# Two cross-attentions: image outputs of all heads added on TensorE to the transposed text outputs

## The chip, the core and the metric

The kernel runs on one core of a Trainium2 chip. The metric is the device time of one execution in microseconds, as the median of repeated runs. The names of the engines in the profile: PE is TensorE's matmuls, PEld its weight loads, DVE is VectorE, ACT is ScalarE, POOL is GpSimd, SP is SyncE, which here only issues DMAs.

## What is computed

Two cross-attention layers run one after the other on 64 batches of 256 positions with 320 channels: 20 heads of 16 channels (D). The context of each batch has 77 tokens of 512 channels. The first layer attends to all 77 text tokens (its image slice is empty); for the second, 73 are text tokens and 4 are image tokens (NIP). In the second layer the image scores also take a cosine between the text-attended context and the image tokens. Cut to the part that the change touches:

```python
text_out = jnp.einsum('bhst,bhtd->bhsd', probs_t, v_t)
...
probs_ip = jax.nn.softmax(fused, axis=-1)
probs_ip = probs_ip * spatial_mask[None, None, :, None]
ip_out = jnp.einsum('bhsn,bhnd->bhsd', probs_ip, v_ip)
...
out = text_out + IP_SCALE * ip_out
out = out @ W_out + b_out
out = out + residual
```

All of it is in float32. The image part of the output is a weighted sum over only four tokens a head.

## The kernel before, in words

Batches go in pairs p (NP = 32 of them, each two batches b of 256 positions). The work of a pair is cut in ten units, five a batch, and one loop of steps g runs everything as a software pipeline: step g belongs to p = g // 10 and k = g % 10. In each step the first layer works on unit g and the second on unit g - 13 (LAG), and its products on the unit before that. All other work (projections, keys, loads, the image part) is a list of "fillers" that the function `fillers(k, p)` hangs on step k. Fillers of the second layer's end belong to pair p - 2. Each step emits, in this order: leftovers of the step before ("drains", kept in `held`), the products and scores into the score banks of PSUM (L769, L776, L654), fillers `begin`, VectorE's maximum and subtraction (L672, L674) for each layer, the transposes of the second layer's weights (L718, L719; copies L725, L726), fillers `first`, the products' sums (L787, L790, copy L1102), the transposes of the first layer's weights (the same L718, L719; copies L744, L745), fillers `second` and `third`. In steps 1, 6 and 8 the sums' copy (L1102) is emitted ahead of the first layer's transposes, in the others behind.

`keep_order` fixes that the instructions of PE, ACT, DVE and POOL run in the order in which they are emitted. SP's order is fixed so for the first 13 steps alone; after that the scheduler of the framework orders the DMA issues.

PSUM has eight banks: four for the scores (`psc`), two for `ptr` (tag "tr") and two for `pms` (tag "ms"). Each pool hands its two buffers out in turn, and a new tile waits until its buffer has been read out.

The path of the image outputs of pair p - 2 before the change:

- `text_output` (POOL, L895 through `by_head`): at the end of a batch (step 9 for b = 0, step 4 for b = 1) it writes the normalized text outputs. Heads 0 to 15 (HT) go to `an`, the last four heads of both batches to `an_last`, positions on the partitions.
- `text_transposed` (steps 0 and 5, `third`): four TensorE transposes of `an` (L856) and two ACT copies (L858) into `aT1`, channels on the partitions.
- `image_weights` (POOL) in steps 2 and 7 makes the image weights `iw` and `iw_last`. `image_transposed` (step 7, L952, copy L954) turns the weights of 16 heads, 64 rows, into `iwT`.
- `image_values` (steps 7 and 8) loads the image values of 16 heads by 16 DMAs a batch (L483), each the same four rows of `vip_rows`; `place_image_values` (POOL, step 9, L488) sets all but each head's own channels to zero.
- `image_attend` (step 8, after the scores): four matmuls a pair (L964), of 32 rows each, into two banks of `pms`; ACT copies them to `ip_out` (L974), POOL adds them to `aT1` (L976; for the last pair VectorE, L972).
- `last_image_values` loads the last four heads' values, broadcast over all partitions (L494); `last_image_outputs` (POOL, steps 4 and 7) multiplies and adds them token by token, eight instructions a batch (L867, L870), onto `an_last`; `last_transposed` (step 8) transposes `an_last` (L877) and ACT copies it (L880).
- `project(1, p - 2)` (step 9, L542) reads `aT1`; its end (L552, L612) follows in step 0.

Other names that the working uses: `value_rows` (L386, copy L387) projects rows of values in steps 6 and 8; `values` loads them back by batch into `vm` and `vr` or `v_rest` (L402), `place_values` spreads them on POOL (L431 to L471); `keys_by_head` (L372) follows it on POOL, and the copy `kT` (L344) waits for that.

Of the kernel before, what the change touches and what calls it, by code (L numbers as in the profile page):

```python
# [14 lines left out]
H = 20  # L15
# [55 lines left out]
def tile_two_cross_attentions(ctx: ExitStack, tc: tile.TileContext, a: dict, out: bass.AP):  # L71
# [182 lines left out]
    ip_mask = blocks("ip_mask", HT * NIP, HT, NIP)  # L254
# [21 lines left out]
    for b in range(2):  # L276
        nc.vector.memset(gv[b][:, :, :, GV - 1 :], 1.0)
        nc.vector.memset(gr[b], 0.0)
        nc.gpsimd.tensor_copy(
            gr[b][:, :, :, GR - 1 :], rest1.unsqueeze(1).unsqueeze(3).broadcast_to([P, 3, 2, 1])  # L280
        )

# [48 lines left out]
    kTs, kbds, qs, vips, aTs = {}, {}, {}, {}, {}  # L331
# [145 lines left out]
    def image_values(p, b):  # L477


        n, r0 = HT * NIP, (2 * p + b) * NIP  # L480
        vip = vips[p, b] = big.tile([n, 2 * P], F32, tag="vip", name=f"vip{p}_{b}", bufs=3)
        for h in range(HT):
            nc.sync.dma_start(vip[h * NIP : (h + 1) * NIP, :], vip_rows[r0 : r0 + NIP, : 2 * P])  # L483

    def place_image_values(p, b):
        n, vip = HT * NIP, vips[p, b]
        v = vip.rearrange("p (h d) -> p h d", d=D)
        nc.gpsimd.tensor_tensor(v, v, ip_mask[:n].unsqueeze(2).broadcast_to([n, HT, D]), ALU.mult)  # L488

    def last_image_values(p, b):  # L490

        r0 = (2 * p + b) * NIP
        v = vips[p, b, "last"] = small.tile([P, NIP, HALF], F32, tag="vlast", name=f"vlast{p}_{b}", bufs=1)
        nc.sync.dma_start(v, vip_rows[r0 : r0 + NIP, 2 * P :].unsqueeze(0).broadcast_to([P, NIP, HALF]))  # L494
# [338 lines left out]
    lasts = {}  # L833

    def text_output(p, b):

        sums = stats[p, b][1]
        rec = small.tile([P, 2 * H], F32, tag="rec", name=f"rec{p}_{b}", bufs=2)
        nc.vector.reciprocal(rec, sums[:, :, NIP + D])
        an = big.tile([P, 2, HT, D], F32, tag="an", name=f"an{p}_{b}", bufs=1)  # L840
        if b == 0:
            lasts[p] = big.tile([P, 2, 2, H - HT, D], F32, tag="an_last", name=f"an_last{p}", bufs=1)
        by_head(an, lasts[p][:, :, b], sums[:, :, NIP : NIP + D], rec)
        return an

    def text_transposed(p, b):

        an = made["an"]
        if b == 0:
            aTs[1, p] = channels("aT1", f"aT1_{p}", 1)  # L850
        main = aTs[1, p][0]
        for s in range(2):
            ps = ptr.tile([P, 4, P], F32, tag="tr", name=f"atr{p}_{b}{s}")
            t = an[:, s].rearrange("p h d -> p (h d)")
            for i in range(2):
                nc.tensor.transpose(ps[:, i, :], t[:, i * P : (i + 1) * P], ident)  # L856
            t0 = b * S + s * P
            nc.scalar.copy(main[:, :, t0 : t0 + P], ps[:, :2])  # L858

    def last_image_outputs(p, b):  # L860

        v = vips[p, b, "last"].rearrange("p t (h d) -> p t h d", d=D)
        w, to = weights[p, b, "last"], lasts[p][:, :, b]
        part = [P, 2, H - HT, D]
        for t in range(NIP):
            prod = small.tile(part, F32, tag="ip_last", name=f"ip_last{p}_{b}{t}", bufs=1)
            nc.gpsimd.tensor_tensor(  # L867
                prod, v[:, t].unsqueeze(1).broadcast_to(part), w[:, :, :, t].unsqueeze(3).broadcast_to(part), ALU.mult
            )
            nc.gpsimd.tensor_add(to, to, prod)  # L870

    def last_transposed(p):

        pool, tag = (ptr, "tr") if p == NP - 1 else (pms, "ms")
        ps = pool.tile([P, 512], F32, tag=tag, name=f"ltr{p}")
        for s in range(2):
            nc.tensor.transpose(  # L877
                ps[:, s * P : (s + 1) * P], lasts[p][:, s].rearrange("p b h d -> p (b h d)"), ident
            )
        nc.scalar.copy(aTs[1, p][1], ps[:, :S])  # L880
# [3 lines left out]
    def by_head(to, last, t, factor):  # L884

        n = t.shape[2]
        for out, at in ((to[:, 0], 0), (last, HT), (to[:, 1], H + 4)):
            m = H - HT if out is last else HT
            full = [P, 2, m, n] if out is last else [P, m, n]
            k = 2 * m if out is last else m  # L890
            x, f = t[:, at : at + k], factor[:, at : at + k]
            if out is last:
                x = x.rearrange("p (s h) d -> p s h d", s=2)
                f = f.rearrange("p (s h) -> p s h", s=2)
            nc.gpsimd.tensor_tensor(out, x, f.unsqueeze(len(full) - 1).broadcast_to(full), ALU.mult)  # L895

# [33 lines left out]
    def image_weights(p, b):  # L930

        num = nums[p, b]
        m = small.tile([P, 2, H], F32, tag="imx", name=f"imx{p}_{b}", bufs=1)
        r = m.rearrange("p s h -> p (s h)")
        nc.vector.tensor_reduce(r, num, AX.X, ALU.add)
        nc.vector.reciprocal(r, r)
        nc.gpsimd.tensor_mul(m, m, smask.unsqueeze(2).broadcast_to([P, 2, H]))
        to = weights[p, b] = small.tile([P, 2, HT, NIP], F32, tag="iw", name=f"iw{p}_{b}", bufs=2)
        last = weights[p, b, "last"] = small.tile(
            [P, 2, H - HT, NIP], F32, tag="iw_last", name=f"iw_last{p}_{b}", bufs=1  # L940
        )
        by_head(to, last, num, r)
# [3 lines left out]
    def image_transposed(p):  # L946
        n = HT * NIP
        ps = ptr.tile([P, 4, P], F32, tag="tr", name=f"itr{p}")
        for b in range(2):
            w = weights[p, b].rearrange("p s h t -> p s (h t)")  # L950
            for s in range(2):
                nc.tensor.transpose(ps[:n, 2 * b + s, :], w[:, s], ident)  # L952
        wT = big.tile([n, S2], F32, tag="iwT", name=f"iwT{p}", bufs=1)
        nc.scalar.copy(wT, ps[:n].rearrange("p j t -> p (j t)"))  # L954
        return wT

    def image_attend(p):

        wT = made["wT"]
        both = [pms.tile([P, 512], F32, tag="ms", name=f"ipv{p}_{i}") for i in range(2)]  # L960
        for b in range(2):
            for i in range(2):
                rows = slice(i * QR, (i + 1) * QR)
                nc.tensor.matmul(  # L964
                    both[i][:, b * S : (b + 1) * S], vips[p, b][rows, i * P : (i + 1) * P],
                    wT[rows, b * S : (b + 1) * S], start=True, stop=True,
                )

        def out_of(i):
            main = aTs[1, p][0]  # L970
            if p == NP - 1:
                nc.vector.tensor_add(main[:, i, :], both[i], main[:, i, :])  # L972
                return
            nc.scalar.copy(t[:, i, :], both[i])  # L974
            if i:
                nc.gpsimd.tensor_add(main, t, main)  # L976

        t = big.tile([P, 2, S2], F32, tag="ip_out", name=f"ip_out{p}", bufs=1)
        return [lambda i=i: out_of(i) for i in range(2)]
# [4 lines left out]
    def fillers(k, p):  # L984


        f = ([], [], [], [])
# [5 lines left out]
        if k == 0:  # L993
# [6 lines left out]
            add(2, p - 2, text_transposed, p - 2, 0)  # L1000
# [3 lines left out]
        elif k == 1:  # L1004
# [5 lines left out]
            add(1, p - 2, last_image_values, p - 2, 0)  # L1010
# [13 lines left out]
        elif k == 3:  # L1024
# [7 lines left out]
            if p - 2 == NP - 1:  # L1032
                add(1, p - 2, last_image_outputs, p - 2, 0)
        elif k == 4:
# [5 lines left out]
            if p - 2 < NP - 1:  # L1040
                add(1, p - 2, last_image_outputs, p - 2, 0)
            add(1, p + 1, queries, 0, p + 1)
        elif k == 5:
# [4 lines left out]
            add(2, p - 2, text_transposed, p - 2, 1)  # L1048
            add(1, p - 2, last_image_values, p - 2, 1)
        elif k == 6:  # L1050
# [9 lines left out]
            add(1, p, place_image_keys, p)  # L1060
        elif k == 7:
# [3 lines left out]
            add(1, p - 2, last_image_outputs, p - 2, 1)  # L1065
            add(1, p - 1, image_values, p - 1, 0)
            if p == 0:
                add(1, p, image_rows)
        elif k == 8:
# [4 lines left out]
            add(1, p - 1, image_values, p - 1, 1)  # L1074
            add(1, p - 1, place_values, 1, p - 1, 1)
            if p - 2 < NP - 1:
                add(1, p - 2, last_transposed, p - 2)
            add(3, p - 2, lambda: held.update(i=lambda: image_attend(p - 2)))
        else:
            add(0, p - 2, project, 1, p - 2)  # L1080
            if p - 2 == NP - 1:
                add(1, p - 2, last_transposed, p - 2)
            add(1, p + 1, values, 0, p + 1, 0)
            for b in range(2):
                add(1, p - 1, place_image_values, p - 1, b)
# [20 lines left out]
    for g in range(NP * NU + LAG + 12):  # L1106
        p, k = divmod(g, NU)
        first, second, third, begin = fillers(k, p)
# [7 lines left out]
        drains = [fn for what in ("q", "o") if what in held for fn in held.pop(what)()]  # L1116
        for fn in drains:
            fn()
        drains = []
# [10 lines left out]
        for fn, args in begin:  # L1130
            fn(*args)
        if "i" in held:
            drains += held.pop("i")()
        for fn in drains:
            fn()
# [44 lines left out]
        if before1:  # L1180
            q, b, u = before1[:3]
            nc.vector.tensor_reduce(eight(stats[q, b][2], u), prod, AX.X, ALU.add)  # L1182
            if ends:
                image_squares(q, b)
                made["an"] = text_output(q, b)
# [70 lines left out]
```

## Time and profile before

| | |
|---|---|
| runs, us | 2484.47, 2491.33, 2488.75; median 2488.75 |
| the profiled execution, us | 2487.73 |
| its span, first to last instruction, us | 2486.0 |
| granted TensorE clock, mean | 0.995 |
| POOL busy in L867, L870, L976, us | 105.7, 116.7, 73.5 |
| POOL busy in the mask L488, us | 38.3 |
| ACT busy in L858, L974, L880, us | 41.9, 33.3, 12.5 |
| PE busy in L856, L964, L877, us | 42.3, 40.6, 12.5 |
| DMA issues of vip and of vlast | 1024 of 4.0 KB, 64 of 128.0 KB |

How to read it: the span is what one execution took by the hardware profiler, about 1.7 us less than its own device time. A line such as "1243.37 1.20 PE L964 MATMUL ipv<-iwT,vip 32*128 32x256 f32 x8" in a timeline gives the start in us from the span's start, the time until the last of the merged instructions ended, the engine, the line of the kernel, output and inputs, the shape, and how many were merged; a bracket at the end is the engine's idle time before it and what ended that. Ends of matmuls overlap with the next ones' starts, so the distance between starts is the better measure. Each float32 matmul appears as two MATMUL instructions, each transpose as one. "SPq" rows are DMA issues in SP's queue.

### The profile page before, as it was taken

How to read it: one execution, taken by the hardware profiler on the slowest of the kernel's cores; microseconds unless marked ns; L12 is line 12 of the kernel's file. 1: busy time of each engine (PE TensorE's matmuls, PEld its weight loads, DVE VectorE, ACT ScalarE, POOL GpSimd, SP SyncE). 2: the span in 40 equal slices, each digit the busy share in tenths (PEclk: the TensorE clock that was granted, in tenths of full speed). 3: DMA queues.
4: the chain of work that ended last, by engine and by line, in shares of the span. 5: the costliest groups of instructions: out<-in, count | busy, mean ns of one | idle time of the engine just before them, and what ended most of it. 6: DMA issues, size and time to landing. Idle time of an engine off the chain costs nothing.

```text
span 2486.0 us, 102184 instructions
## 1 busy us (share of the span) xinstructions
PE 2414.7 (97%) x40990; PEld 1857.7 (75%) x40990; DVE 1974.2 (79%) x3673; ACT 1506.3 (61%) x3893; POOL 1635.7 (66%) x3962
## 2 busy tenths in 40 slices
PE   8999999999999999999999999999999999999898
PEld 5677777777777777777777777777777777777676
DVE  3588788888887888888888887888887888888864
ACT  3466666666665666666666665665665666666643
POOL 2467676676666776666676676676675676676654
PEclk9999999999999999999999999999999999999999
DMA  5212121212221212121122211122211222211100
GB/s 172 60 48 58 57 58 47 60 56 60 57 59 41 62 56 61 57 60 51 51 63 58 66 48 51 49 59 60 59 57 41 59 57 61 64 46 40 33 27 28
DMA packets 186511, 140.08 MB, mean 56 GB/s; under 512 B 81016, under 2 KB 164728, under 8 KB 186040
## 3 DMA queue, kind: packets, MB, share of 16 engines
q1 hardware_dynamic: 185176, 132.41, 18.9%
q8 instruction: 325, 5.32, 0.9%
q10 hardware_dynamic: 864, 1.15, 0.2%
q14 instruction: 146, 1.20, 0.2%
HBM read 95.56 MB, written 33.91 MB: 52 GB/s over the span
## 4 chain that ended last, share of the span: by engine, by line
PE 65%; DVE 13%; POOL 6%; ACT 5%; DMA 5%; SPq 4%; issue 3%; DVEq 0%; POOLq 0%; ACTq 0%
PE tr L718 8%; PE sc L769 7%; PE o_ps L542 7%; PE sc L654 5%; PE q_ps L542 4%; DVE w L674 4%; PE v_ps L386 4%; PE sc L776 3%; PE o_ps L627 3%; PE k_ps L341 3%; PE pv L804 3%; DVE mx L672 2%; PE pv L809 2%; PE o_ps L552 2%; ACT w L682 2%
## 5 line engine op out<-in xcount | busy, mean ns | idle before, releaser
L672 DVE TENSOR_REDUCE mx<-sc 128x8 f32<-128x584 f32 (+1 forms) x640 | 497.0, 777 | 363.9 <-PE sc L654 362.6
L705 POOL TENSOR_TENSOR parts<-w,sm 128x512 f32<-128x512 f32 (+1 forms) x640 | 440.4, 709 | 344.1 <-ACT parts L686 139.6
L674 DVE TENSOR_TENSOR w<-sc,mx 128x616 f32<-128x616 f32 x640 | 512.0, 800 | 72.7 <-POOL an L895 0.9
L718 PE MATMUL tr<-ident,parts 128*128 128x128 f32 x2560 | 408.8, 282 | 8.0 <-POOL parts L705 3.1
L718 PEld LDWEIGHTS tr<-ident,parts 128*128 128x128 f32 x2560 | 285.0, 141 | 131.1 <-issue 75.7
L725 ACT COPY pt<-tr 128x512 f32<-128x512 f32 x320 | 187.7, 586 | 285.1 <-PE tr L718 282.1
L682 ACT ACTIVATE w<-w 128x616 f32<-128x616 f32 x320 | 231.2, 722 | 123.9 <-DVE w L674 123.0
L769 PEld LDWEIGHTS sc<-gv,pt 64*64 64x64 f32 x10240 | 233.2, 133 | 81.7 <-ACT sums L1102 42.6
L769 PE MATMUL sc<-gv,pt 64*64 64x94 f32 x10240 | 277.4, 245 | 13.5 <-ACT sums L1102 12.6
L700 DVE TENSOR_REDUCE sm<-w 128x8 f32<-128x616 f32 x320 | 251.2, 785 | 13.8 <-ACT w L682 13.8
L542 PE MATMUL q_ps<-x,wq 128*128 128x256 f32 x1024 | 238.2, 384 | 17.3 <-ACT kT L344 16.9
L654 PE MATMUL sc<-kbd,q 32*64 32x154 f32 x10240 | 249.9, 294 | 1.1 <-ACT q L597 1.0
L542 PE MATMUL o_ps<-aT,wo 128*128 128x256 f32 x1024 | 231.8, 379 | 0.3 <-DVE aT L972 0.3
L1182 DVE TENSOR_REDUCE nrm<-prod 128x8 f32<-128x584 f32 x320 | 226.8, 709 | 0.3
L542 PEld LDWEIGHTS q_ps<-x,wq 128*128 128x128 f32 x1024 | 190.4, 192 | 45.5 <-ACT kT L344 22.4
L1102 ACT COPY sums<-sc 128x168 f32<-128x168 f32 x320 | 96.5, 302 | 205.2 <-DVE prod L790 202.9
L787 DVE TENSOR_TENSOR prod<-sc,parts 128x512 f32<-128x512 f32 x320 | 218.2, 682 | 2.8 <-PE sc L776 2.8
L542 PEld LDWEIGHTS o_ps<-aT,wo 128*128 128x128 f32 x1024 | 189.6, 190 | 24.0 <-DVE aT L972 0.7
L685 ACT ACTIVATE parts<-w 128x512 f32<-128x512 f32 x320 | 207.4, 648 | 0.0
L744 ACT COPY pt<-tr 128x512 f32<-128x512 f32 x256 | 150.9, 590 | 66.9 <-PE tr L718 66.3
L386 PE MATMUL v_ps<-wv,cf 128*128 128x320 f32 (+1 forms) x624 | 181.8, 438 | 0.0
L719 PE MATMUL rtr<-ident,parts 128*104 128x128 f32 (+1 forms) x640 | 174.9, 273 | 0.0
(147 smaller groups left out, 4734.9 us busy)
## 6 DMA issues: line engine op xcount, KB each, us to landing
vip<-vip_rows SPq DMA_DIRECT2D x1024, 4.0 KB
out_dram<-x SPq DMA_DIRECT2D x64, 256.0 KB
x<-in_x_dram SPq DMA_DIRECT2D x31, 512.0 KB
v_rows<-vs SPq DMA_DIRECT2D x38, 320.0 KB
vm<-v_rows SPq DMA_DIRECT2D x152, 80.0 KB
ct<-in_ctx_dram SPq DMA_DIRECT2D x32, 308.0 KB
cf<-in_ctx_dram SPq DMA_DIRECT2D x38, 256.0 KB
g_rest<-gram_rest SPq DMA_DIRECT2D x512, 0.5 KB
```

The lines of the kernel that those rows point to most:

```text
L386: nc.tensor.matmul(ps[:n, :C], cfs[i][:, k, :n], wv[l][:, k, :], start=(k == 0), stop=(k == KE - 1))
L542: nc.tensor.matmul(ps[b][:, m, :], w[:, k, m * P : (m + 1) * P], main[:, k, b * S : (b + 1) * S], start=(k == 0 and m == 0), stop=False,)
L654: nc.tensor.matmul(ps[c, r, 2 * T * l : 2 * T * (l + 1)], tokens[rows, c], kbd[rows, part].rearrange("p e t -> p (e t)"), start=start, sto ...
L672: nc.vector.tensor_reduce(mx, sc[:, :, :, :nt], AX.X, ALU.max)
L674: nc.vector.tensor_tensor(w, sc, mx.unsqueeze(3).broadcast_to([P, 4, 2, T]), ALU.subtract)
L682: nc.scalar.activation(w, w, AF.Exp, scale=SCALE)
L700: nc.vector.tensor_reduce(sm, w, AX.X, ALU.add)
L705: nc.gpsimd.tensor_tensor(two[:, 8 * t0 : 8 * t1].rearrange("p (h t) -> p h t", h=8), w[:, :, t0:t1], sm.unsqueeze(2).broadcast_to([P, 8, ...
L718: nc.tensor.transpose(ps[:, i, :], flat[:, i * P : (i + 1) * P], ident)
L769: nc.tensor.matmul(ps[c, i % 2 * 2 + j, at : at + GV], pt[half_rows, i, c], gv[b][half_rows, part, i, :], start=start and i < 2, stop=False,)
L787: nc.vector.tensor_tensor(prod[:, :, :, :M], sm[:, :, :, :M], w[:, :4].rearrange("p (e a) j t -> p (a j) e t", e=2), ALU.mult)
L1182: nc.vector.tensor_reduce(eight(stats[q, b][2], u), prod, AX.X, ALU.add)
```

## The change

The image outputs of all 20 heads are now computed by TensorE and added in PSUM onto the transposed text outputs. One function, `outputs(p - 2)`, run as the last filler of step 8, replaces `text_transposed`, `last_image_outputs`, `last_transposed` and `image_attend`. It takes both `pms` banks and one `ptr` bank. TensorE transposes the text outputs of both batches into the `pms` banks (eight) and the last heads' into the `ptr` bank (two), with the bank cleared by the first one alone; then six matmuls (three blocks of rows a batch: 32, 32 and 16) add the image outputs. Three ACT copies to `aT1` are held and emitted at the head of step 9.

For this, `an` exists once a batch; the image weights stand in one tile of 20 heads and are transposed with 80 rows instead of 64; the values of a batch are in a fixed tile `vips[b]` of 80 rows, loaded by two DMAs a batch in step 9 and masked on POOL in step 6 of the pair after, by two instructions a batch. GpSimd makes no image outputs any more. The last pair is treated as the others.

The diff, cut to its core:

```diff
-    ip_mask = blocks("ip_mask", HT * NIP, HT, NIP)
+    ip_mask = blocks("ip_mask", H * NIP, H, NIP)
...
+    vips = [const.tile([H * NIP, 2 * P], F32, tag=f"vip{b}", name=f"vip{b}") for b in range(2)]
+    for t in vips:
+        nc.vector.memset(t[HT * NIP :], 0.0)
...
     def image_values(p, b):
-        vip = vips[p, b] = big.tile([n, 2 * P], F32, tag="vip", name=f"vip{p}_{b}", bufs=3)
-        for h in range(HT):
-            nc.sync.dma_start(vip[h * NIP : (h + 1) * NIP, :], vip_rows[r0 : r0 + NIP, : 2 * P])
...
+        rows = vip_rows[r0 : r0 + NIP, :].unsqueeze(0)
+        nc.sync.dma_start(
+            vips[b][:n], rows[:, :, : 2 * P].broadcast_to([HT, NIP, 2 * P])
+        )
+        nc.sync.dma_start(
+            vips[b][n:, b * HALF : (b + 1) * HALF],
+            rows[:, :, 2 * P :].broadcast_to([H - HT, NIP, HALF]),
+        )
+
+    def place_image_values(b):
+        n = HT * NIP
+        for rows, c0, heads in ((slice(0, n), 0, slice(0, HT)), (slice(n, H * NIP), b * HALF, slice(HT, H))):
+            m = heads.stop - heads.start
+            v = vips[b][rows, c0 : c0 + m * D].rearrange("p (h d) -> p h d", d=D)
+            mask = ip_mask[rows, heads].unsqueeze(2).broadcast_to([rows.stop - rows.start, m, D])
+            nc.gpsimd.tensor_tensor(v, v, mask, ALU.mult)
...
-            nc.gpsimd.tensor_tensor(
-                prod, v[:, t].unsqueeze(1).broadcast_to(part), w[:, :, :, t].unsqueeze(3).broadcast_to(part), ALU.mult
-            )
-            nc.gpsimd.tensor_add(to, to, prod)
...
-    def image_attend(p):
+    def outputs(p):
 
         wT = made["wT"]
-        both = [pms.tile([P, 512], F32, tag="ms", name=f"ipv{p}_{i}") for i in range(2)]
+        main, last = aTs[1, p] = channels("aT1", f"aT1_{p}", 1)
+        both = [pms.tile([P, 512], F32, tag="ms", name=f"atr{p}_{i}") for i in range(2)]
+        third = ptr.tile([P, 4, P], F32, tag="tr", name=f"ltr{p}").rearrange("p j t -> p (j t)")
+
+        def turned(to, rows, first):
+            nc.tensor.matmul(to, rows, ident, is_transpose=True, start=first, stop=False, skip_group_check=True)
+
+        for i in range(2):
+            for b in range(2):
+                for s in range(2):
+                    rows = ans[b][:, s].rearrange("p h d -> p (h d)")[:, i * P : (i + 1) * P]
+                    turned(both[i][:, b * S + s * P : b * S + (s + 1) * P], rows, b == s == 0)
+        for s in range(2):
+            turned(third[:, s * P : (s + 1) * P], lasts[p][:, s].rearrange("p b h d -> p (b h d)"), s == 0)
         for b in range(2):
-            for i in range(2):
-                rows = slice(i * QR, (i + 1) * QR)
+            for i in range(3):
+                rows = slice(i * QR, min((i + 1) * QR, H * NIP))
                 nc.tensor.matmul(
-                    both[i][:, b * S : (b + 1) * S], vips[p, b][rows, i * P : (i + 1) * P],
-                    wT[rows, b * S : (b + 1) * S], start=True, stop=True,
+                    both[i][:, b * S : (b + 1) * S] if i < 2 else third[:, :S],
+                    vips[b][rows, i * P : (i + 1) * P] if i < 2 else vips[b][rows, :P],
+                    wT[rows, b * S : (b + 1) * S], start=False, stop=b == 1, skip_group_check=True,
                 )
...
-            nc.scalar.copy(t[:, i, :], both[i])
-            if i:
-                nc.gpsimd.tensor_add(main, t, main)
...
+        return lambda: [lambda i=i: nc.scalar.copy(main[:, i, :], both[i]) for i in range(2)] + [
+            lambda: nc.scalar.copy(last, third[:, :S])
+        ]
...
-            add(2, p - 2, text_transposed, p - 2, 0)
...
+            for b in range(2):
+                add(1, p - 2, place_image_values, b)
...
-            if p - 2 < NP - 1:
-                add(1, p - 2, last_transposed, p - 2)
-            add(3, p - 2, lambda: held.update(i=lambda: image_attend(p - 2)))
+            add(2, p - 2, lambda: held.update(i=outputs(p - 2)))
...
             for b in range(2):
-                add(1, p - 1, place_image_values, p - 1, b)
+                add(1, p - 1, image_values, p - 1, b)
...
-        drains = [fn for what in ("q", "o") if what in held for fn in held.pop(what)()]
+        drains = [fn for what in ("i", "q", "o") if what in held for fn in held.pop(what)()]
```

## The prediction

> **What bounds the kernel now.** I read the page first (busy shares, chain), then the waits, then the timelines of one pair of batches engine by engine.
>
> ```profile
> PE 2414.7 (97%) x40990; PEld 1857.7 (75%) x40990; DVE 1974.2 (79%) x3673; ACT 1506.3 (61%) x3893; POOL 1635.7 (66%) x3962
> PE 65%; DVE 13%; POOL 6%; ACT 5%; DMA 5%; SPq 4%; issue 3%; DVEq 0%; POOLq 0%; ACTq 0%
> ```
>
> TensorE is busy for 97% of the span and holds 65% of the chain. POOL, which the change relieves, holds 6%. A busy share says little where matmuls overlap, so the steps decide. A step runs from one start of L672's 616-column maximum on VectorE to the next. In the median over the pairs, steps 0 to 9 of a pair take 7.48, 7.32, 7.01, 8.83, 8.22, 6.42, 6.53, 6.53, 6.60 and 7.79 us. Two things can end a step: TensorE's own work, or the loop from the scores through VectorE's five passes and the copy of the sums (L1102) back to the next products (L769). The loop has a floor: in step 5 the scores are there at 1223.96 and the sums' copy ends at 1228.36, 4.40 us later; products and scores then take 1.79. That makes 6.2 us, the length step 5 has in the pairs where it is shortest.
>
> The PE timeline of steps 5 and 6 shows both cases:
>
> ```profile
> 1228.00 0.66 PE L856 MATMUL atr<-ident,an 128*128 128x128 f32 x4
> 1228.59 0.88 PE L769 MATMUL sc<-gv,pt 64*64 64x94 f32 x32
> ...
> 1235.06 0.88 PE L769 MATMUL sc<-gv,pt 64*64 64x94 f32 x32 [0.34 <-ACT sums L1102]
> ```
>
> In step 5 the text transposes fill TensorE until the products start, 0.19 us later than the loop would allow (1228.40). In step 6 TensorE sits idle 0.34 us for the loop. All other steps show no such idle time: TensorE sets them. The step that matters is 8 (PE, then ACT):
>
> ```profile
> 1243.37 1.20 PE L964 MATMUL ipv<-iwT,vip 32*128 32x256 f32 x8
> 1244.49 0.66 PE L718 MATMUL tr<-ident,parts 128*128 128x128 f32 x4
> 1244.98 0.27 PE L719 MATMUL rtr<-ident,parts 128*128 128x128 f32 x1
> 1245.17 2.42 PE L386 MATMUL v_ps<-wv,cf 128*128 128x320 f32 x8
> 1247.42 0.60 PE L718 MATMUL tr<-ident,parts 128*128 128x128 f32 x4
> 1247.86 0.27 PE L719 MATMUL rtr<-ident,parts 128*104 128x128 f32 x1
> 1247.97 0.38 PE L877 MATMUL ltr<-ident,an_last 128*128 128x128 f32 x2
> 1248.30 0.88 PE L769 MATMUL sc<-gv,pt 64*64 64x94 f32 x32
> ```
>
> ```profile
> 1247.94 0.30 ACT L1102 COPY sums<-sc 128x168 f32<-128x168 f32 x1
> 1248.13 0.60 ACT L744 COPY pt<-tr 128x512 f32<-128x512 f32 x1
> ```
>
> There is no hole on PE, so whatever is added to this step lengthens it.
>
> **GpSimd's part.** It loses eight L867 (413 ns) and eight L870 (456 ns) a pair, 6.95 us, and one L976 of 2.37 us; it gains two small masks, taken at the 286 ns of L445's 32x64 form. That is 8.7 us of POOL a pair. I price it at nothing: in the view of L867, TensorE waits for it 2.1 us in all, its weight loads 11.4 us, nearly all hidden behind running matmuls. In step 9 L776 waits 0.24 us for POOL's L451 in the pair at 1250; over the run that wait sums to a few us. The masks move into step 6, ahead of the image weights: those end 1.8 us later, at 1240.3 instead of 1238.5. The weights' transposes start at 1240.14 with the first batch, long ready; the second batch's turn is 0.2 us later. Cost 0, at most 0.2 us a pair.
>
> **ScalarE's part.** Four copies of 386 ns a pair (L858) go; the other three keep their sizes and move to the head of step 9. They wait for the new block, and behind them in ACT's queue stands L725, which needs transposes that come 1.7 us of products and scores later. The copies take about 1.5 us (586, 586, 390, overlapping a little). L542 needs them too, 2.3 us after the products start, so 0.8 us of cover is left.
>
> **TensorE's part**, step by step.
> Steps 0 and 5 lose four transposes each. In step 0 L856 starts at 1190.20 and L769 at 1190.79, and the sums were out at 1189.48: 0.59 goes, less a switch of matmul shapes, so -0.55. In step 5 the loop takes over: -0.19. Together -0.74 us.
> Step 8 loses L964 (1243.37 to 1244.49: 1.12) and L877 with its switch (1247.97 to 1248.30: 0.33). It gains, at its end, ten transposes and six two-pass matmuls. Five transposes take 0.55 us (1247.42 to 1247.97), so ten take 1.1, and 0.1 for the switch. Four image matmuls take 1.12 us, 0.28 each with their start; the third block's two more cost 0.24 each by the spacing inside the row: 1.6. The ends of that price: 1.12, if three row groups run side by side and the third is free; 2.6, if each of twelve passes takes the 0.216 of L542's (16 passes from 1250.57 to 1254.03). I take 1.6, from the same kind of matmul. Sum without any wait: 2.8 - 1.45 = +1.36.
> The Trainium skill (TensorE: Matmul & The Clock Gate, Part 3, "Measured speedup vs the span model") says that matmuls on different row groups overlap at about 4 ns a tile. By it the third block is nearly free, and the forecast would be some 14 us lower. The row's eight passes at 1.12 us show two groups overlapping at best, so I stay with the row.
>
> **The added wait.** The last block's transposes go into the pool `ptr` with two buffers, as its third tile after tr and rtr of the same step. So they wait until ACT's L744 has emptied tr. In step 8 the sums' copy stands ahead of L744, and VectorE's L790 ends at 1247.56 whatever TensorE does. With L974 and L880 gone ACT can copy the sums at once, and L744 ends 0.79 after their start (1247.94 to 1248.73 now): 1248.37. TensorE would come there earlier: 1243.37, plus 0.68 and 2.25 and 0.55 for the rows above, plus 0.88 for eight transposes: 1247.73. So it stands 0.7 us, with the image matmuls queued behind. The same kind of wait is on record in step 7, where the weights' transposes (itr) are ptr's third tile and the view of L744 has their loads waiting for it 11 times. Bounds: 0, if it is met in time, and 0.8. Where step 8 projects two blocks of value rows (8.8 us steps, 6 of 30 pairs), TensorE comes 2.2 us later and nothing waits.
> So step 8 grows by 2.06 us in 24 pairs and by 1.36 in 6: 57.6 us. Steps 0 and 5 give back 30 x 0.74 = 22.2.
>
> **SyncE's queue.** 1024 small loads of vip and 64 of vlast become four a pair.
>
> ```profile
> 1879.16 3.67 SPq L483 DMA_DIRECT2D vip<-vip_rows  x11
> 1882.94 1.31 SPq L402 DMA_DIRECT2D vm<-v_rows  x4
> ```
>
> ```profile
> 1891.86 0.72 POOL L460 TENSOR_TENSOR v<-vm,half 128x320 f32<-128x320 f32 x1 [7.91 <-DMA v_rest<-v_rows]
> ```
>
> ```profile
> 1894.54 2.07 PE L542 MATMUL q_ps<-x,wq 128*128 128x256 f32 x4 [4.42 <-ACT kT L344]
> ```
>
> POOL freed vm's buffer at 1879.47, but eleven vip issues stood in SP's queue ahead of the next vm load. It went out 3.5 us late, POOL waited, and TensorE idled 4.42 us in step 4. Step 4 exceeds 8.22 us in 13 pairs, by 25.4 us in all. Taking in each pair the smaller of the excess and the issue's delay beyond 0.4 us (the pairs without vip ahead show 0.03 to 0.8) gives 14 us. The rest is the slow landing itself, which stays. Bounds: 0, if other loads take the place, and 25.4. L494's waits (327.7 us in SP's list) go too, but SP runs ahead there and TensorE is not late after them. The new loads wait for the image matmuls of step 8, done before POOL frees vm in step 9, so they hold up nothing.
>
> **The end.** After the last weights TensorE's ten transposes hide behind the copy of iwT, but the results then need ACT copies (586 each) where VectorE added in 0.69, and six matmuls instead of four: L542 starts 1.4 later. The present 0.46 wait for ltr's copy and its 0.38 then go: +0.6.
>
> **Sum.** 57.6 - 22.2 - 14 + 0.6 = +22 us on the profiled execution's 2487.7 (span 2486.0): 2510. That execution lies 1 us under the median 2488.75, so no correction is made.
>
> **Rivals.**
> (a) Forecast: step 8 pays for block and wait, 2500 to 2522. Chance 0.52.
> (b) The wait for L744 doesn't come. For it: it rests on 0.7 us of timing. Against: VectorE's 1247.56 is fixed by the loop. 2510 - 24 x 0.7 = 2493, on the edge of what can be told from no change. 0.22, half each.
> (c) Untiled passes: the third block of 16 rows breaks the overlap, 2.6 for 1.6: 2510 + 30 = 2540. Against: L964's own rows. 0.13.
> (d) Faster, by the SP queue: with 10.7 us of vip issue a pair gone (32 at 3.67 / 11) every late value load vanishes, -25.4 instead of -14. It decides only if the block is cheap as well, at most 0.9 us net in step 8 (third row group free, no wait): 30 x 0.88 - 22.2 - 25.4 = -21, so 2467. For it: 13 late pairs. Against: loads that start at once still land late (step 4 was 1.85 over with an issue 0.7 after the buffer was free). 0.13, of which 0.02 ends within 0.3%.
> That POOL's relief does nothing at all is part of (a).
>
> Within 0.3% is about what a measurement of this kernel can tell from no change. Slower: 0.52 + 0.11 + 0.13 = 0.76. Same: 0.11 + 0.02 = 0.13. Faster 0.11. The range leaves out the faster case and the far half of (c), 0.17: 2484 to 2535.
>
> **What would show it.** Right: step 8 near 8.6 us, with TensorE idle 0.7 before the third tile's transposes and the releaser ACT pt; step 0 near 6.9 and step 5 near 6.2; step 4 over 8.3 us in fewer pairs; POOL near 1360 us busy with no step shorter for it. Wrong: step 8 under 7.5 us (block cheaper), TensorE idle in step 9 before the output projection L542 (copies late), image weights' transposes late in step 7, or step 4 as long as now.

## The result and the profile after

The changed kernel takes 2497.53 us (2494.62 to 2497.9, 8 runs); the kernel before, in the same set, 2488.87 (2484.47 to 2493.73, 8 runs). The ratio is 1.0031 with a 95% interval of 1.002 to 1.0042: slower by 8.7 us, where 22 were forecast. The profiled span is 2496.2 us (2486.0 before), the granted clock 0.997 (0.995). That the clock is no lower matters: the difference is work and waits, not pace.

The page of the changed kernel, the lines on busy time and on the chain:

```profile
PE 2401.9 (96%) x41118; PEld 1849.4 (74%) x41118; DVE 1987.1 (80%) x3673; ACT 1479.6 (59%) x3767; POOL 1371.7 (55%) x3483
PE 75%; DVE 15%; ACT 4%; DMA 2%; issue 2%; POOL 1%; SPq 0%; DVEq 0%; POOLq 0%; ACTq 0%
```

GpSimd lost 264 us of busy time, and its share of the chain went from 6% to 1%; SP's queue went from 4% to nothing. The freed share of the chain is TensorE's now. The lines of the code moved by some five: the maximum that marks a step is L677 now, tr L723, the first layer's copy L749, the sums' copy L1057. New are the block's transposes L928, the image matmuls L940, the copies L945 and L946.

The steps of a pair, as in the prediction from one start of the 616-column maximum to the next, in us. The first three columns are medians over the pairs, the last is the difference summed over pairs 2 to 30:

| step | before | after | sum of differences |
|---|---|---|---|
| 0 | 7.48 | 6.35 | -28.0 |
| 4 | 8.22 | 8.22 | -18.9 |
| 5 | 6.42 | 6.25 | -2.5 |
| 7 | 6.53 | 6.73 | +4.7 |
| 8 | 6.60 | 8.17 | +39.7 |
| 9 | 7.79 | 8.31 | +11.9 |
| 1, 2, 3, 6 | 7.32, 7.01, 8.83, 6.53 | the same | -0.3 |

These make +6.6 us. Pairs 0 and 1, the start, pair 31 and the end add 3.5. Steps 9 and 0 belong together, since the mark between them shifted: -28.0 and +11.9 make -16.1.

Step 8 on TensorE in the changed kernel, first the block alone:

```profile
1251.36 1.04 PE L928 MATMUL atr<-ident,an 128*128 128x128 f32 x8
1253.13 0.44 PE L928 MATMUL ltr<-ident,an_last 128*128 128x128 f32 x2 [0.73 <-ACT pt L749]
1253.49 0.48 PE L940 MATMUL atr<-iwT,vip 32*128 32x256 f32 x2
...
1254.56 0.88 PE L774 MATMUL sc<-gv,pt 64*64 64x94 f32 x32
```

The bracket on the second line is the added wait: after eight transposes TensorE idles 0.73 us, until ACT's copy L749 has emptied tr. Then the last two transposes run, the six image matmuls take 1.07 us (1253.49 to 1254.56), and the products follow. ACT in the same stretch:

```profile
1252.29 0.30 ACT L1057 COPY sums<-sc 128x168 f32<-128x168 f32 x1 [0.85 <-DVE prod L795]
1252.48 0.59 ACT L749 COPY pt<-tr 128x512 f32<-128x512 f32 x1
```

ACT stands idle 0.85 us for VectorE's sums, with L749 queued behind the copy of the sums. So VectorE holds TensorE up, through the order of two copies on ACT. The first experiment tests that.

### The profile page after: what moved, and what is told of

Same layout as the page of the kernel before. It is cut to its first block, busy times and chain, and to the rows that moved or that the text cites. A ratio compares the mean times of both kernels' runs of the same rounds, so it can differ in the third digit from the quotient of the medians.

```text
span 2496.2 us, 100470 instructions
## 1 busy us (share of the span) xinstructions
PE 2401.9 (96%) x41118; PEld 1849.4 (74%) x41118; DVE 1987.1 (80%) x3673; ACT 1479.6 (59%) x3767; POOL 1371.7 (55%) x3483
## 4 chain that ended last, share of the span: by engine, by line
PE 75%; DVE 15%; ACT 4%; DMA 2%; issue 2%; POOL 1%; SPq 0%; DVEq 0%; POOLq 0%; ACTq 0%
PE sc L774 9%; PE tr L723 9%; PE o_ps L547 8%; PE q_ps L547 8%; PE sc L659 7%; DVE w L679 6%; DVE mx L677 4%; PE sc L781 4%; PE o_ps L632 3%; PE k_ps L345 3%; PE pv L809 3%; PE v_ps L390 2%; PE o_ps L557 2%; DVE prod L792 2%; PE q_ps L557 2%; PE q_ps L575 2%
## 5 line engine op out<-in xcount | busy, mean ns | idle before, releaser
L677 DVE TENSOR_REDUCE mx<-sc 128x8 f32<-128x584 f32 (+1 forms) x640 | 496.9, 776 | 365.1 <-PE sc L659 362.2
L723 PE MATMUL tr<-ident,parts 128*128 128x128 f32 x2560 | 408.1, 282 | 9.5 <-ACT pt L730 5.6
L723 PEld LDWEIGHTS tr<-ident,parts 128*128 128x128 f32 x2560 | 284.7, 141 | 128.7 <-issue 83.2
L694 POOL COPY att<-w 128x32 f32<-128x32 f32 x320 | 67.0, 210 | 356.6 <-DVE w L679 352.9
L1057 ACT COPY sums<-sc 128x168 f32<-128x168 f32 x320 | 96.2, 300 | 245.0 <-DVE prod L795 245.0
L547 PE MATMUL q_ps<-x,wq 128*128 128x256 f32 x1024 | 232.7, 380 | 5.3 <-ACT kT L348 5.3
L749 ACT COPY pt<-tr 128x512 f32<-128x512 f32 x256 | 150.6, 588 | 66.4 <-PE tr L723 65.3
```

Source lines behind the costliest of these rows:

```text
L547: nc.tensor.matmul(ps[b][:, m, :], w[:, k, m * P : (m + 1) * P], main[:, k, b * S : (b + 1) * S], start=(k == 0 and m == 0), stop=False,)
L677: nc.vector.tensor_reduce(mx, sc[:, :, :, :nt], AX.X, ALU.max)
L723: nc.tensor.transpose(ps[:, i, :], flat[:, i * P : (i + 1) * P], ident)
```

## The experiments

Ratios are against runs of the kernel before on the same chip. Over the sets its median moved between 2485.66 and 2498.98 us, so times of different sets are not subtracted from each other; why it moves was not found.

### The wait in step 8: the sums' copy later

Step 8 is taken out of the two conditions that put the sums' copy ahead of the first layer's transposes:

```diff
-        if before1 and k in (1, 6, 8):
+        if before1 and k in (1, 6):
...
-        if before1 and k not in (1, 6, 8):
+        if before1 and k not in (1, 6):
```

> The changed kernel, but in step 8 the sums' copy is emitted after the first layer's transposes' copies, so ACT empties tr as soon as it is there. Theory (the 0.73 us on PE in front of the last heads' transposes is the wait for L749, and L749 waits behind the sums' copy): step 8 goes from 8.17 to about 7.45 us in some 24 pairs, 17 us in all, 2497.5 to about 2480; the 9.4 us steps with two blocks of value rows stay. Rival (VectorE's loop or the sums would end the step anyway): no change, 2494 to 2500.

Measured: 2477.02 us (2474.88 to 2478.45), ratio 0.9917 (0.9902 to 0.9932). TensorE in step 8:

```profile
1244.66 1.04 PE L928 MATMUL atr<-ident,an 128*128 128x128 f32 x8
1245.54 0.38 PE L928 MATMUL ltr<-ident,an_last 128*128 128x128 f32 x2
1245.85 0.48 PE L940 MATMUL atr<-iwT,vip 32*128 32x256 f32 x2
...
1246.92 0.88 PE L774 MATMUL sc<-gv,pt 64*64 64x94 f32 x32
```

No bracket is left: ten transposes take 1.19 us, the matmuls 1.07 as before, the block 2.26 instead of 3.20. ACT now empties tr first:

```profile
1244.75 0.59 ACT L749 COPY pt<-tr 128x512 f32<-128x512 f32 x1
...
1245.59 0.30 ACT L1057 COPY sums<-sc 128x168 f32<-128x168 f32 x1
```

Step 8 went from 8.17 to 7.22 us in the pairs with one block of value rows, and stayed at 9.38 in the six with two, as the prediction had said of them (there TensorE comes later and does not wait). The steps of pairs 2 to 30 sum to 2142.8 us instead of 2161.2. The wait is shown as cause, at 0.95 us in each pair with one block: 0.73 idle and some 0.2 for starting again.

### The price of the image matmuls: two blocks, one block

The image matmuls of a batch work on three blocks of rows, 32, 32 and 16. Each block, by the rows that its records show (32*128 or 16*128), is called a row group here. A pass is one MATMUL record, and a float32 matmul has two. Here the changed kernel runs with fewer of the three blocks; first with two:

```diff
-            for i in range(3):
+            for i in range(2):
```

> The changed kernel without the third block of image matmuls: the last four heads get no image outputs. Theory (three row groups run side by side and the third is free, as 1.07 us for twelve passes say): no change, 2495 to 2500. Rival (the price of the prediction, 0.24 us a matmul): 0.48 us a pair, 14 us less, about 2483.

Measured: 2499.97 us (2497.85 to 2501.91), ratio 1.0007 (0.9995 to 1.0019); step 8 8.17 us, unchanged. The third block was free, against the 0.48 us that the prediction had put on it. Then one (`range(1)`):

> The changed kernel with only the first of the three image matmul blocks of a batch (the heads of the second and third block are left without image outputs). Theory (the row groups work beside each other, and what costs is the passes of one group, some 1.07 us from the first start of the image matmuls to the first product): step 8 stays at 8.17 us within 0.1, and the total within 4 us of the changed kernel, since the accumulating block has the price of one group whatever the number of groups up to three. Rival (two groups share the array's time and only the third was free): the image matmuls take half, step 8 falls by 0.4 to 0.55 us to some 7.7, 12 to 16 us less in all, a ratio of about 0.995 to the kernel before.

Measured: 2499.52 us (2497.29 to 2503.31), ratio 1.0003 (0.9993 to 1.0013); step 8 8.16 us. TensorE:

```profile
1256.52 1.13 PE L940 MATMUL atr<-iwT,vip 32*128 32x256 f32 x4
1257.58 0.88 PE L774 MATMUL sc<-gv,pt 64*64 64x94 f32 x32
```

Four passes of one row group take 1.06 us from start to start; eight passes of two groups took 1.12 in the kernel before, twelve of three 1.07. The price is that of one group; the second and the third beside it add nothing that shows.

### The masks, in another step

`place_image_values` moved from step 6 to step 5, after the filler `gram`:

```diff
+            for b in range(2):
+                add(1, p - 2, place_image_values, b)
...
-            for b in range(2):
-                add(1, p - 2, place_image_values, b)
```

> The changed kernel with the masks of the image values on POOL in step 5 instead of step 6. Theory (step 7 grew by 0.2 us because the masks hold up the last image weights): step 7 back from 6.73 to 6.53 us, 29 pairs, 5 us, and up to 1.6 us at the end, where the masks stand ahead of the last pair's weights: about 2491. Rival (step 7 grew for the 80-row weights or another reason): no change, 2495 to 2500.

What it is about, on POOL of the changed kernel, and on PE:

```profile
1241.94 1.99 POOL L499 TENSOR_TENSOR vip<-vip,ip_mask 64x256 f32<-64x256 f32 x4
1244.01 0.25 POOL L903 TENSOR_TENSOR imx<-imx,smask 128x40 f32<-128x40 f32 x1
1244.34 0.75 POOL L862 TENSOR_TENSOR iw<-num,imx 128x64 f32<-128x64 f32 x3
```

```profile
1244.59 0.86 PE L915 MATMUL itr<-ident,iw 128*80 128x128 f32 x4
```

Four transposes from 1244.59 use weights that POOL finishes at 1245.09, after 1.99 us of masks. Measured: 2497.07 us (2494.88 to 2498.53), ratio 0.9998 (0.9989 to 1.0008). Step 7 fell from 6.73 to 6.54, as far as it stood before the change, so its +4.7 us is the masks' doing. The steps of pairs 2 to 30 sum to 2158.2 instead of 2161.2. In the whole time that is too little to show; the 2491 us that was expected did not come.

Both edits together:

> The changed kernel with both edits: in step 8 the sums' copy behind the first layer's transposes' copies, and the masks in step 5. Theory: the two savings add, 20 us by the first and some 5 by the second: ratio to the kernel before about 0.993 against 1.003 of the changed kernel, step 8 at 7.2 and step 7 at 6.54 us. Rival (the masks' saving doesn't reach the end of the run): the same as the first edit alone, a further 0 us.

Measured: 2472.41 us (2469.39 to 2474.83), ratio 0.9896 (0.9879 to 0.9912); step 8 7.22, step 7 6.54, pairs 2 to 30 in 2137.5 us. In the steps the savings add; in the whole time the second is too small to be told from the first alone (0.9917).

### SyncE's queue: small loads put back, and taken from the kernel before

The changed kernel with the rows of the 16 heads loaded one head at a time again:

```diff
-        nc.sync.dma_start(
-            vips[b][:n], rows[:, :, : 2 * P].broadcast_to([HT, NIP, 2 * P])
-        )
+        for h in range(HT):
+            nc.sync.dma_start(vips[b][h * NIP : (h + 1) * NIP, :], vip_rows[r0 : r0 + NIP, : 2 * P])
```

> The changed kernel with 16 loads of four rows a batch for the first 16 heads' image values again, as before the change, at the place of the new load (30 more issues a pair on SP). Here they stand behind the last projection of value rows and not ahead of the value loads of step 2. Theory P (what mattered was the place in SP's queue, ahead of a load that TensorE needs): step 4 stays short, 2495 to 2501. Rival N (what mattered was the number of loads and SP's issue time): step 4 is long again in some ten pairs, 14 to 19 us more, 2511 to 2517.

Measured: 2603.21 us (2597.36 to 2610.34), ratio 1.0431 (1.0407 to 1.0456): far beyond both expectations. Step 4 has a median of 10.15 us and lies 91.5 us over 8.22 in sum. DMA issues on SP in that run:

```profile
1240.23 4.21 SPq L486 DMA_DIRECT2D vip<-vip_rows  x12
1244.53 0.69 SPq L487 DMA_DIRECT2D vip<-vip_rows  x1
1245.32 5.47 SPq L486 DMA_DIRECT2D vip<-vip_rows  x16
...
1271.51 1.54 SPq L406 DMA_DIRECT2D vm<-v_rows  x4
```

The sixteen issues take 5.47 us, 0.34 each. The fixed tiles of the changed kernel come free only after the image matmuls of step 8, so these loads go out in a burst, and all behind them is late, the value loads of step 2 by 2.6 to 7.3 us in pairs 3 to 30. In the kernel before, the same number stood spread over steps. So the count alone isn't the price; count and place are.

The other way round, the kernel before with one load a batch for the 16 heads, and nothing else changed:

```diff
-        for h in range(HT):
-            nc.sync.dma_start(vip[h * NIP : (h + 1) * NIP, :], vip_rows[r0 : r0 + NIP, : 2 * P])
+        nc.sync.dma_start(
+            vip, vip_rows[r0 : r0 + NIP, : 2 * P].unsqueeze(0).broadcast_to([HT, NIP, 2 * P])
+        )
```

> The kernel before with one load a batch of the 16 heads' image values in place of 16 small ones; nothing else is changed. Theory (the small loads' issues in SP's queue, 0.34 us each, make the value load of step 2 late, and that alone gave the changed kernel back 19 us in step 4): step 4's excess over 8.22 us falls from 25 to about 6 us, the other steps stay: 17 to 21 us less than before, ratio about 0.992. Rival (step 4 got shorter because POOL was relieved): no change, ratio 0.998 to 1.002.

Measured: 2468.31 us (2465.83 to 2472.27), ratio 0.9876 (0.9858 to 0.9894). The waits of SP's queue, of the kernel before and of this one (total, times, longest):

```profile
SPq L402 <- POOL gv L437: 19.8, 11, 8.2
```

```profile
SPq L402 <- POOL gv L437: 236.5, 63, 9.2
```

L402 are the value loads, and more waiting is good here: SP stands ready 63 times for POOL to free the buffer, instead of coming late. From pair 1 on each value load of step 2 goes out 0.03 us after its buffer is free (0.03 to 5.9 before). What step 4 has over 8.22 us fell from 25.4 to 6.4 us, the value of the changed kernel; the other steps stayed. Pairs 2 to 30 take 2137.4 us, against 2154.6 before. This part of the change, alone, beats the change and needs nothing of its block. Once more in another set:

> The kernel before with one load for the replicated image-value rows, once more, beside the kernel without GpSimd's last heads, on the same chip. Theory: ratio 0.986 to 0.990 as in the first run of it (0.9876), a value load issued within 0.1 us of its buffer's release in every pair. Rival (the first run drew a lucky chip state, and the queue's share is the 14 us of the prediction): ratio 0.992 to 0.996.

Measured: 2464.97 us (2464.14 to 2467.07), ratio 0.9918 (0.9903 to 0.9933), between the two bands; from pair 1 on the value loads go out within 0.1 us and the steps of pairs 2 to 30 sum to 2134.2, as the theory has it. It was the kernel before that differed: 2485.66 us here, 2496.95 there.

### GpSimd's relief

The kernel before without the eight instructions a batch on POOL that add the image outputs of the last four heads:

```diff
-        for t in range(NIP):
+        for t in range(0):
```

> The kernel before without the sixteen multiplications and additions a pair on POOL for the last four heads, whose image outputs are left out; all loads stay. Theory (POOL is not on the path): POOL some 220 us less busy, the steps as before, 0 to 4 us less at the most, ratio 0.998 to 1.001. Rival (POOL's 6% of the chain are worth something): a gain of over 10 us, ratio under 0.996.

Measured: 2568.41 us (2567.05 to 2575.42), ratio 1.0286 (1.0265 to 1.0306). Less work, 2.9% slower: neither theory had that. The same edit on the kernel with one load:

> The kernel before with the image-value rows replicated by one load for all heads, and without GpSimd's image outputs of the last four heads (their part of the output is left out: the text outputs alone stand there). The load stays. The run of the kernel before without that GpSimd work but with its sixteen small loads came out 2.9% slower, with unchanged step medians and late value loads, so it did not price the work. Here the loads cannot get in the way. Theory (the 264 us of GpSimd work that the change takes off are worth nothing on the path): median steps as in the kernel before with one load (7.28, 7.32, 7.01, 8.83, 8.22, 6.42, 6.47, 6.53, 6.60, 7.72) within 0.1 us each, a ratio of 0.986 to 0.990. Rival (the relief is worth 10 us or more, hidden until now by the queue of loads): ratio at or under 0.983, with steps 0, 1 and 9 shorter by 0.3 us or more a pair. Second rival (the same slowdown by another order of the loads): ratio over 1.0, value loads issued late again and step 4 over 8.22 us in most pairs.

Measured: 2558.93 us (2557.16 to 2559.64), ratio 1.0241 (1.0226 to 1.0256). Both lose in pairs 1 to 4 alone, in single steps of up to 32 us; in pairs 8 to 30 this run takes 1690.9 us and the kernel with one load 1696.2. (The expectation's steps for the kernel with one load are those of the run with the small loads; its own are 7.48 in step 0 and 7.81 in step 9, so the relief shows in this run's 7.28 and 7.72.) In the same pairs the run before it, with the small loads, takes 1697.1 us against 1713.4 of the kernel before, 12.2 of the difference in step 4: the sixteen loads are still there and make less late. What they cost depends on what else stands in the queue. SP in pair 1 of this run, and its wait list over the run:

```profile
119.11 10.60 SPq L495 DMA_DIRECT2D vlast<-vip_rows  x4
...
140.37 16.89 SPq L495 DMA_DIRECT2D vlast<-vip_rows  x6
```

```profile
SPq L495 <- DMA vlast<-vip_rows: 147.7, 54, 4.0
```

The loads of the last heads' values were left in. Nobody reads them any more, so nothing spreads them: they move up in SP's order and each waits, at the head of the queue, for the one before it in the same buffer. Six of them hold the queue for 16.89 us. To test that, these loads went too:

```diff
-        v = vips[p, b, "last"] = small.tile([P, NIP, HALF], F32, tag="vlast", name=f"vlast{p}_{b}", bufs=1)
-        nc.sync.dma_start(v, vip_rows[r0 : r0 + NIP, 2 * P :].unsqueeze(0).broadcast_to([P, NIP, HALF]))
```

> The kernel before with one load for the replicated image-value rows, without GpSimd's image outputs of the last four heads and without the loads that fed them (the image part of these four heads is left out of the output). The two runs without that GpSimd work lost their time in pairs 1 to 4 alone: there loads that nobody reads any more stood in SyncE's queue and waited for one another (54 waits, 148 us in the second of the two). In pairs 8 to 30 that run took 1690.9 us and the one with the GpSimd work 1696.2. Theory (the slowdown came from the dead loads, and GpSimd's relief is worth 0.23 us a pair): pairs 1 to 4 as in the kernel before with one load, a ratio 0.002 to 0.004 under that run's, 0.984 to 0.987 by the earlier set. Rival (the GpSimd work spread the other loads, and without it the start goes wrong whatever is loaded): ratio over 1.0 again, with steps 2, 4, 8 or 9 of pairs 1 to 4 over 13 us.

Measured: 2458.78 us (2457.07 to 2463.1), ratio 0.9898 (0.988 to 0.9916), 0.002 under the kernel with one load in the same set, 6.2 us in medians. Pairs 1 to 4 are back to normal. So the dead loads made the slowdown, and the last heads' work on GpSimd, with its loads, is worth about 6 us: step 0 went from 7.48 to 7.28, step 9 from 7.78 to 7.72. It is not nothing, though with four runs of each the two intervals overlap; the steps are the better evidence.

### The changed kernel again

> The changed kernel itself, beside the other runs of this set, so that they can be compared on one chip: 0.3% over the kernel before, as on record.

Measured: 2499.99 us (2498.04 to 2504.1), ratio 1.0011 (1.0 to 1.0021). The medians of the steps are those of the table within 0.03 us, step 4 is 11.3 us over 8.22 in sum (6.4 in the first trace). On this chip the kernel before took 2496.95. Its one trace is from another set, so why the ratio moves is not shown.

## Why the prediction was too high

The direction was right, the size more than double: 22 us for 8.7 in medians and 10 in the traces. Term by term, in the traces: step 8 came some 16 us under its price and the queue gave 5 more; steps 0 and 5, the masks and the end together came some 11 over. The other 2 us are the start and the last pair, which the table's sums leave out.

**The step that failed** is the price of the six image matmuls in "TensorE's part": "the third block's two more cost 0.24 each by the spacing inside the row: 1.6". They take 1.07, and 0.53 us in 30 pairs is 16 us. In the 29 pairs of the table step 8 grew by 39.7 us where the prediction's prices make 55.5; the matmuls are nearly all of that gap. The row of L964, eight passes in 1.12 us, was read as eight passes of 0.14, and so as two groups that overlap in part. It was four passes of 0.28 with the second group free beside them: one group alone takes 1.06. The lower end given, 1.12 with "the third is free", was the true case. So was the rule of the Trainium skill (TensorE: Matmul & The Clock Gate, Part 3, "Measured speedup vs the span model"), by which a further row group costs some 4 ns; the prediction set it aside. The runs agree with it: 1.06, 1.12 and 1.07 us for one, two and three groups.

**Step 8 otherwise.** The wait was forecast at 0.7 us and came at 0.73, for the reason given; with TensorE starting again it is worth 0.95. Ten transposes were priced 1.2 with their switch and take 1.19. The value rows and the tr transposes came out 0.09 and 0.08 us shorter than taken. In all 1.57 us a pair instead of 2.06, and 0.63 instead of 1.36 with two blocks of value rows.

**Steps 0 and 5** were to give back 22.2 us, 0.55 and 0.19 a pair. Step 0, with step 9, gave 16.1 in 29 pairs, 0.56 each; step 5 gave 2.5. It reached the loop's 6.25, but 13 of the 29 pairs were within 0.1 us of that already. That step 0 came out is luck in part: two things that nobody had priced cancel there. TensorE gained some 0.3 us a pair by GpSimd's relief (below), and lost about as much, most of it as a stand before the matmuls L512, whose weight loads wait 8.7 us over the run, 2.3 before.

**SyncE's queue** was put at 14 us, with 11.4 to stay as slow landing. 18.9 went and 6.4 stayed. The slow landing did stay: in pair 10 it is 9.0 us from issue to use in both traces. What the prediction left out is TensorE's pace after a long stand. Step 4 of pair 10, before and after:

```profile
777.38 3.20 PE L542 MATMUL q_ps<-x,wq 128*128 128x256 f32 x8 [2.77 <-ACT kT L344]
```

```profile
778.70 1.99 PE L547 MATMUL q_ps<-x,wq 128*128 128x256 f32 x8 [1.16 <-ACT kT L348]
```

The same eight matmuls take 3.20 us after 2.77 us of idling, at a granted clock of 0.60 (777.4 to 780.6 us), and 1.99 after 1.16. In the kernel before, pairs 10, 20 and 25 idle 2.77, 2.74 and 4.42 us there, and the clock of step 4 is 0.87 to 0.88; in the other late pairs, with idles up to 2.38 us, it is 1.00. TensorE is busy 1.5 to 1.6 us longer in each of the three, which is nearly the 4.9 us between 14 and 18.9. The queue is the part with the largest gain, 17 to 20 us in the steps of the kernel before with one load.

**The masks** were priced 0, with 0.2 us a pair as the most; they cost 0.2 in step 7 of the pairs with one block, 4.7 us. The prediction looked at when the weights end, and allowed 1.8 us; the second batch's transposes were late by the little that it named.

**The end.** Pair 31 and what follows cost 4.3 us more, against 0.6. Most of it is in steps 7 and 8 of pair 31, which take 19.28 us instead of 15.63. No value rows are projected there, and the added wait of step 8 is the longer for it:

```profile
2374.44 0.44 PE L928 MATMUL ltr<-ident,an_last 128*128 128x128 f32 x2 [1.98 <-ACT pt L749]
```

In the two runs with the sums' copy later, these two steps take 17.77 and 17.37 us. How the rest divides was not found; the granted clock is 0.82 in step 7 there, where before it was 0.79 in step 8. Behind the steps the last pair has the same masks in it, with nothing beside them. POOL and PE of the changed kernel there:

```profile
2475.51 2.02 POOL L499 TENSOR_TENSOR vip<-vip,ip_mask 64x256 f32<-64x256 f32 x4
```

```profile
2478.49 0.56 PE L915 MATMUL itr<-ident,iw 128*80 128x128 f32 x2 [2.77 <-POOL iw L862]
...
2481.85 0.79 PE L940 MATMUL atr<-iwT,vip 32*128 32x256 f32 x2
...
2484.38 3.72 PE L547 MATMUL o_ps<-aT,wo 128*128 128x256 f32 x16 [0.67 <-ACT aT L945]
```

The 2.77 us that TensorE waits for the weights are not the price of the masks. From POOL's first text output of the last unit to the last weights it takes 7.46 us, 6.63 before, so the masks delay the weights by some 0.8. With the masks in step 5 it is 8.28 and TensorE waits 3.58: there they stand ahead of another instruction of POOL on the same path, and the saving that was expected at the end does not come. From the weights to the output projection it takes 5.70 us, 3.23 before: 2.5 more, where the prediction had 1.4. The image matmuls alone take 1.9 us for 1.07, at a granted clock of 0.50 (2481.85 to 2483.30): their starts follow each other by 0.43 us, in step 8 by 0.21.

**GpSimd's relief** was put at nothing. In the kernel before the last heads' part is worth about 6 us, 0.2 a pair. It is not the 11.4 us in which weight loads wait for L867: without L867 the loads of the text transposes wait as long, 11.9 us, for another instruction of POOL (L688 in that run). It is the other wait that the prediction named, of the products L776 for POOL's L451 at the end of step 9, taken there for a few us in all and priced at nothing. Before and after:

```profile
1256.57 0.44 PE L776 MATMUL sc<-gr,pr 32*64 32x60 f32 x12
1257.25 0.27 PE L776 MATMUL sc<-gr,pr 32*64 32x60 f32 x2 [0.24 <-POOL gr L451]
```

```profile
1262.83 0.37 PE L781 MATMUL sc<-gr,pr 32*64 32x60 f32 x16
```

From the first products there to the next transposes TensorE takes 1.98 us in the median before, and 1.67 both in the changed kernel and in the run without the last heads' work and loads (1.96 in the kernel with one load beside it). So the changed kernel has this gain too, within steps 9 and 0 of the table.

**Rivals.** The time came near rival (b)'s 2493, but not in its way: the wait was there. Rival (c) fell, with its reason: the third block breaks no overlap. Rival (d) had both its conditions half right, the block cheaper and more gained in SP's queue, and it lacked the wait: with that taken away, the changed kernel is 0.8% faster than the kernel before. That POOL's relief does nothing, part of rival (a), is not so.

**What the change is worth.** With its two faults mended, by both edits, it takes 2472.41 us, and the kernel before with one load 2468.31 in the same set, whose steps sum to 2137.5 and 2137.4. So the mended form, with all of GpSimd's image outputs gone, is no faster than the old one with one edit on its loads. Against that old form its steps 0 and 5 sum to 28.6 and 4.1 us less, 8 and 9 to 18.2 and 13.1 more. So what the mended change gains over the kernel before it owes to the loads; the rest, GpSimd's relief included, comes out even.

## What to carry to other kernels

Price small matmuls on row groups by the passes of one group (measured here for up to three): read a row of overlapping instructions per group, not per record. When work moves to a busy engine, look for the cheap side effect that rides along (here fewer DMA issues), and try it alone. When an instruction's reader goes, take its loads out as well: loads that nobody waits for still hold a queue. When a long stand goes, count the pace behind it as well as the stand.

## What the runs showed of the chip

A queue of DMA issues blocks in order: a load that waits for the buffer of the load before it holds all behind it (16.89 us for six). That fits the Trainium skill (DMA: Bandwidth & Descriptors, "Anatomy of one DMA — SWDGE (gpsimd) path"), which says that a wait on a semaphore happens on the issuing sequencer before dispatch; the section is on DMAs that GpSimd issues, while these are issued by SP.

What step 4 still loses in the changed kernel falls on pairs 6, 10, 21 and 25: their value loads are issued 0.03 us after the buffer is free, but POOL can use them only 9.0 to 9.5 us after. From pair 2 on, most pairs have them by the time POOL comes, after 4.4 us. In the four late pairs the 64 rows of the second batch cross a block of 128 rows and are loaded in pieces of 23 and 41 or of 17 and 47 rows, all prime; pairs 11 and 20, with 43 and 21, take 7.6 and 7.2. By the Trainium skill (DMA: Bandwidth & Descriptors, "Why a DMA increments its semaphore by 16 and not by 1") a load runs on the largest number of DMA engines up to 16 that divides the slowest dimension of both its sides, here its rows, which is one engine for these. The trace fits: while the rows of pair 21 land (1586.0 to 1594.3 us), the mean busy share of the 16 DMA engines is 0.10, little more than one of them; in pair 9, whose 64 rows are not split, it is 0.23 (694.0 to 697.5). The other splits, 49 and 15 or 39 and 25 for example, show 4.4 like the whole loads, 45 and 19 up to 4.9. No run with another split was made, so the cause is argued, not shown.
